# The preparation of a four-layer convolution kernel: projection by column and by row in two strips of 64 array rows

## The chip, the core and the metric

The kernel runs on one core of one Trainium2 chip. A core has five engines that run their own instruction streams: TensorE (matmuls), VectorE, ScalarE, GpSimd and SyncE, which here only issues DMA transfers. The metric is the device time of one execution in microseconds (us); lower is better. Three executions of the kernel before took 5565.35, 5569.03 and 5571.29 us, with a median of 5569.03.

## What is computed

The input x has shape (2, 128, 128, 128): two images, 128 channels, 128 rows, 128 columns, all float32. Four layers follow each other, each as x + layer(group norm of x): an axial attention with relative positions, four directional recurrent convolutions, a deformable convolution, and a Hadamard-transformed convolution. Only the preparation of the first layer is touched. Cut to that part, the reference is:

```python
x = jnp.transpose(x, (0, 3, 1, 2))          # (N, W, C, H)
x = x.reshape(N * W, C, H)                  # one sequence for each column of an image
# qkv: a grouped projection, 8 groups, 16 input and 32 output channels in each group
# q, k: 8 channels of a group each, v: 16; each followed by batch norms whose
# statistics run over all sequences and positions
```

The attention scores of a group are the sum of q·k and of two products with a table of relative positions. Each of the three is normalised with its own mean and variance over all sequences and positions. The preparation must therefore find these moments before the attention can start, and it must leave q, k and v behind in device memory.

## The kernel before, in words

`layer0_prepare` (L92) keeps both images in on-chip memory as `xa[n]`, with the 128 channels on the partitions and rows x columns (128 x 128) along the free dimension. The projection weights are block-diagonal: output channel of group g uses only the 16 input channels of group g. `wt` holds them as columns: 256 to 383 are q and k (64 q columns, then 64 k columns, 8 for each group in turn), 384 to 511 are v (16 for each group).

First the images arrive, their Gram matrices are summed, and the group norm and batch norm are folded into the weights. From L295 a loop over k (0: q and k, 1: v) broadcasts the scales and biases to all partitions (`rows`, L304) and makes the folded weights `wz[n]` (L307) on VectorE.

Then two stages follow, each a loop of turns over tiles of RT = 4 columns or rows:

- **By column** (L361 to L452, 64 turns: 2 images x 32). `sequences` (L371) multiplies, for each of 4 columns, the image column `xa[n][:, :, w]` as stationary operand (128 channels x 128 rows; neighbouring rows lie 128 elements apart) by the folded weights (256 columns: q, k, v). VectorE adds the biases while it takes the results out of PSUM: q and k go to `zb`, v goes to `vs`, which is written to device memory every fourth turn. `moments` (L400) multiplies `zb` by itself in 16 small matmuls of 32 columns; ScalarE copies one half of the result, VectorE multiplies it by the other, GpSimd sums up.
- **By row** (L456 to L569, 33 turns). `positions` (L466) multiplies, for each of 4 rows and both images, the image row `xa[n][:, h, :]` (128 elements side by side) by the q and k weights (128 columns). VectorE adds the bias into `zt`. `against_embeddings` (L489) multiplies `zt` by itself in 32 small matmuls into `pg`, which VectorE multiplies by the table `eg`. From turn 4 on, `project` (L512) also writes q and k themselves: the weights are stationary, 16 x 32 pixels move, ScalarE takes the result out twice (`sa`, `sb`), and SyncE writes it to device memory.

TensorE, VectorE and ScalarE go through a wrapper `InOrder` (L73), whose line 81 is therefore the line of nearly all instructions in the profile; the program's order is kept on each engine. In each column turn the order is: matmuls of `sequences` for turn i, then `moments` of turn i - 1. In each row turn: `positions` of turn t, the share of `project`, then `against_embeddings` of turn t - 1. GpSimd's and SyncE's instructions are placed by a scheduler.

[...] By column: `ps_zb` 4 x 1 bank, `ps_m` 2, one for small results. By row: `ps_zt` 2 x 1, `pg` 2, `ps_q` 2, one for small results.

Of the kernel before, what the change touches and what calls it, by code (L numbers as in the profile page):

```python
# [7 lines left out]
F32 = mybir.dt.float32  # L8
I32 = mybir.dt.int32
AF = mybir.ActivationFunctionType  # L10
ALU = mybir.AluOpType
# [4 lines left out]
P = 128  # L16
N = 2
S = 128
RT = 4
# [4 lines left out]
NG = 8  # L24
# [67 lines left out]
def layer0_prepare(env, x, prm, mem, alphas):  # L92
# [4 lines left out]

    nc, tc = env.nc, env.tc  # L100
    HW = WC // 2
    with ExitStack() as ctx:
        xpool = ctx.enter_context(tc.tile_pool(name="l0x", bufs=1, side="right"))
        kp = ctx.enter_context(tc.tile_pool(name="l0k", bufs=1))
        xa = [xpool.tile([P, S, S], F32, name=f"xa{n}", tag=f"xa{n}") for n in range(N)]
        pe, dve, act = (InOrder(tc, e) for e in (nc.tensor, nc.vector, nc.scalar))
# [2 lines left out]
        strip, ones = late[:, 0:128], late[:, 128:256]  # L109
        gsim = kp.tile([P, NG, 3], F32, name="gsim", tag="gsim")  # L110
        rows = kp.tile([P, 2, 1 + N, P], F32, name="rows", tag="rows")
        wz = [kp.tile([P, 2, P], F32, name=f"wz{n}", tag=f"wz{n}") for n in range(N)]
        shift = kp.tile([P, N], F32, name="shift_qk", tag="shift_qk")
        eg = kp.tile([P, 9, S], F32, name="eg", tag="eg")

        with ExitStack() as early:
            wp = early.enter_context(tc.tile_pool(name="l0w", bufs=1))
            pp = early.enter_context(tc.tile_pool(name="l0ps", bufs=1, space=PSUM))
            ct = wp.tile([P, 512], F32, name="ct", tag="ct")
            wt = wp.tile([P, 512], F32, name="wt", tag="wt")  # L120
# [57 lines left out]
            a, b, width = e0, e1, 255  # L178
            for k in range(7):
                step = 1 << k  # L180
                width -= step
                to = eg if k == 6 else b
# [3 lines left out]
                a, b = b, a  # L186
# [24 lines left out]
            ps = pp.tile([P, 2 * N], F32, name="psg_l0", tag="ps_small")  # L211
# [83 lines left out]
            for k in range(2):  # L295
                psr = pp.tile([P, 1 + N, P], F32, name="psr", tag="psr")
                for s in range(2):
                    dgs = wp.tile([P, 1 + N, P], F32, name="dgs", tag="dgs", bufs=2)
                    for c in range(1 + N):
                        nc.vector.tensor_scalar(  # L300
                            dgs[:, c, :], pick[:, k, s, :], cols[:, s, c : c + 1], None, ALU.mult
                        )
                    nc.tensor.matmul(psr, lhsT=ones, rhs=dgs, start=(s == 0), stop=(s == 1))
                nc.scalar.copy(rows[:, k], psr)  # L304
                lo = 256 + 128 * k
                for n in range(N):
                    nc.vector.scalar_tensor_tensor(  # L307
                        wz[n][:, k, :],
                        wt[:, lo : lo + P],
                        gs[:, n : n + 1],  # L310
                        rows[:, k, 0, :],
                        ALU.mult,
                        ALU.mult,
                    )
# [30 lines left out]
        def along(n, k, shape):  # L345
            return (
                rows[:, k, 1 + n, :]
                .rearrange("p (b c) -> p b c", b=(4, NG)[k])
                .unsqueeze(1 if k == 0 else 2)
                .to_broadcast(shape)  # L350
            )
# [9 lines left out]
        with ExitStack() as part:  # L361
# [2 lines left out]
            pp = part.enter_context(tc.tile_pool(name="l0pm", bufs=2, space=PSUM))  # L364
            acc = sp.tile([P, 2, 33], F32, name="acc2", tag="acc2")
            nc.gpsimd.memset(acc, 0.0)
            zb = [sp.tile([P, RT, 4, 33], F32, name=f"zb{j}", tag=f"zb{j}") for j in range(2)]
            for t in zb:
                nc.gpsimd.memset(t[:, :, :, 32:33], 1.0)

            def sequences(i, vs):  # L371

                n, w = i // NT, i % NT * RT
                z = zb[i % 2]
                for hf in range(2):
# [9 lines left out]
                    dve.tensor_tensor(  # L385
                        z[:, 2 * hf : 2 * hf + 2, :, 0:32],
                        ps[:, :, 0, :].rearrange("p w (b c) -> p w b c", b=4),
                        along(n, 0, [P, 2, 4, 32]),
                        ALU.add,
                    )  # L390
                    at = (w + 2 * hf) % HW
                    dve.tensor_tensor(
                        vs[:, :, at : at + 2, :],
                        ps[:, :, 1, :].rearrange("p w (g c) -> p g w c", g=NG),
                        along(n, 1, [P, NG, 2, 16]),
                        ALU.add,
                    )
                return z

            def moments(z):  # L400


                ps = pp.tile([P, 2, 2, 33], F32, name="ps_m", tag="ps_m")
                for half in range(2):
                    for b in range(2):
                        for s in range(4):
                            w, block = 2 * half + s // 2, 2 * b + s % 2
# [12 lines left out]
            z_last = None  # L420
            for i in range(N * NT + 1):
# [34 lines left out]
        with ExitStack() as part:  # L456
# [5 lines left out]
            zt = [sp.tile([P, RT, 4, 33], F32, name=f"zt{j}", tag=f"zt{j}") for j in range(4)]  # L462
            for t in zt:
                nc.gpsimd.memset(t[:, :, :, 32:33], 1.0)

            def positions(t):  # L466

                zs = []
                for n in range(N):
                    z = zt[2 * (t % 2) + n]  # L470
                    ps = pp.tile([P, RT, P], F32, name="ps_zt", tag="ps_zt")
                    for hh in range(RT):
                        pe.matmul(
                            ps[:, hh, :],
                            lhsT=xa[n][:, t * RT + hh, :],
                            rhs=wz[n][:, 0, :],
                            start=True,
                            stop=True,
                        )
                    dve.tensor_tensor(  # L480
                        z[:, :, :, 0:32],
                        ps.rearrange("p h (b c) -> p h b c", b=4),
                        along(n, 0, [P, RT, 4, 32]),
                        ALU.add,
                    )
                    zs.append(z)
                return zs

            def against_embeddings(t, zs):  # L489
                pg = pp.tile([P, RT, 33], F32, name="pg", tag="pg")  # L490
                for hh in range(RT):
                    for n in range(N):
                        for b in range(4):
                            pe.matmul(
                                pg[32 * b : 32 * b + 32, hh, :],
                                lhsT=zs[n][:, hh, b, 0:32],
                                rhs=zs[n][:, hh, b, :],
                                start=(n == 0),
                                stop=(n == N - 1),
                            )  # L500
# [1643 lines left out]
```

## Time and profile before

| what | value |
| --- | --- |
| median of 3 runs | 5569.03 us |
| profiled execution, its own time | 5575.76 us |
| profiled execution, span of its instructions | 5574.0 us |
| TensorE matmuls (PE), busy | 5231.2 us, 94% |
| TensorE weight loads (PEld), busy | 4656.9 us, 84% |
| VectorE (DVE), busy | 3700.6 us, 66% |
| ScalarE (ACT), busy | 2582.8 us, 46% |
| GpSimd (POOL), busy | 1532.4 us, 27% |
| stage by column | 112 to 272 us |
| stage by row | 272 to 423 us |

In the rows of a profile, PE is a matmul record and PEld the weight load that goes with it. One float32 matmul of the program leaves two records of each. "128*128 128x256" means a stationary operand of 128 rows and 128 columns and a moving operand of 256 elements on 128 partitions. Matmuls are pipelined, and the duration of a record includes the time through the array, so the distance from one record's start to the next says more than its duration. A timeline row gives the start, the time from the first start to the last end, the engine, the line, the operation, output<-inputs, the shape and the number of records; in brackets the idle time before it and what ended it. In a tile view the durations are minimum/median/maximum in ns.

### The profile page before, as it was taken

To read this page: it belongs to the slowest core of one execution; us is meant where nothing else is said; L and a number is where in the kernel's file an instruction comes from. 1 tells how busy PE (TensorE), PEld (TensorE's weight loads), DVE (VectorE), ACT (ScalarE), POOL (GpSimd) and SP (SyncE) were. 2 spreads that over 40 slices of the span, in tenths; PEclk is the share of its full clock that TensorE was granted. 3 is DMA by queue.
4 is the path that set the end of the run, shared out by engine and by line. 5 is a ranking of instruction groups with operands and counts; after the bars stand their busy time and mean duration, and the time that the engine had idled before them with its cause. 6 is when DMAs were issued, how large, how long until landed. Compare 5 with 4: busy or idle time off the path is not lost. (4 is left out here: it accounts for less than half of the span.)

```text
span 5574.0 us, 171601 instructions
## 1 busy us (share of the span) xinstructions
PE 5231.2 (94%) x71931; PEld 4656.9 (84%) x71931; DVE 3700.6 (66%) x7132; ACT 2582.8 (46%) x7864; POOL 1532.4 (27%) x1169
## 2 busy tenths in 40 slices
PE   7997999999999806999999999999899999999999
PEld 6866888888888706999999999993699999999877
DVE  3635888888888875555555556663466666666798
ACT  1056988898889743443223330003233333333322
POOL 2114666666666621000000003330000000000376
PEclk8998999999999958999999999999999999999999
DMA  3353333333333389900000000104576777766211
GB/s 152 108 221 85 60 60 60 60 60 61 60 60 63 95 338 186 100 1 1 1 1 1 1 1 32 47 16 119 113 87 89 88 85 88 90 88 88 44 50 58
DMA packets 673352, 420.99 MB, mean 76 GB/s; under 512 B 325696, under 2 KB 630720, under 8 KB 660672
## 3 DMA queue, kind: packets, MB, share of 16 engines
q1 hardware_dynamic: 667406, 400.69, 38.9%
q8 instruction: 576, 9.44, 0.7%
q10 hardware_dynamic: 5170, 9.23, 0.5%
q14 instruction: 200, 1.64, 0.1%
HBM read 269.09 MB, written 157.45 MB: 77 GB/s over the span
## 5 line engine op out<-in xcount | busy, mean ns | idle before, releaser
L81 PE MATMUL pl<-ln,wl 128*128 128x128 f32 (+1 forms) x10160 | 1243.3, 276 | 31.3 <-DVE ln L81 29.9
L81 PEld LDWEIGHTS pl<-ln,wl 128*128 128x128 f32 x10160 | 1178.4, 191 | 43.8 <-ACT c L81 21.3
L81 ACT ACTIVATE e<-e,mx 128x128 f32<-128x128 f32 x2048 | 793.4, 395 | 0.8 <-DVE mx L81 0.8
L81 ACT COPY sm<-ps_s 128x432 f32<-128x432 f32 (+1 forms) x768 | 318.4, 487 | 834.1 <-PE ps_s L81 808.8
L81 POOL TENSOR_TENSOR e<-e,total 128x1024 f32<-128x1024 f32 x256 | 485.8, 1897 | 485.5 <-DVE total L81 474.8
L81 ACT COPY res<-ln 128x128 f32<-128x128 f32 x762 | 261.8, 344 | 747.0 <-DVE ln L81 722.0
L81 DVE COPY s<-ps_w 100x1152 f32<-100x1152 f32 x256 | 346.4, 1353 | 334.6 <-PE ps_w L81 334.6
L81 PE MATMUL ps_s<-s,xw 100*128 100x144 f32 x4096 | 546.8, 287 | 7.6 <-DMA xw<-px_d 7.6
L81 POOL TENSOR_TENSOR res<-ln,x1t 128x128 f32<-128x128 f32 x256 | 149.1, 583 | 1456.0 <-DVE ln L81 1456.0
L81 PE MATMUL po<-sm,wdef 128*128 128x256 f32 x2304 | 539.1, 379 | 0.0
L81 PE MATMUL pl<-ln,ws 128*128 128x128 f32 x4064 | 537.6, 274 | 0.0
L81 POOL COPY et<-et 128x1024 f32<-128x1024 f32 x256 | 516.8, 2019 | 34.9 <-DVE et L81 25.7
L81 PEld LDWEIGHTS ps_s<-s,xw 100*128 100x128 f32 x4096 | 518.7, 191 | 8.2 <-DMA xw<-px_d 8.0
L81 DVE TENSOR_TENSOR v<-pl,c 128x128 f32<-128x128 f32 x508 | 148.0, 291 | 564.8 <-PE pl L81 542.3
L81 PEld LDWEIGHTS pl<-ln,ws 128*128 128x128 f32 x4064 | 495.5, 191 | 0.0
L81 ACT ACTIVATE r<-gen,alphas 128x1536 f32<-128x1536 f32 x256 | 395.0, 1543 | 171.3 <-PE gen L81 142.4
L81 PEld LDWEIGHTS po<-sm,wdef 128*128 128x128 f32 x2304 | 419.8, 190 | 47.7
L81 POOL MEMSET col<- 128x10 f32 (+1 forms) x72 | 5.9, 122 | 1462.0 <-DVE res L81 1454.6
L81 ACT ACTIVATION_READ_ACCUMULATOR e<-e,mx 128x1 f32 x2048 | 396.2, 193 | 0.0
L81 DVE SCALAR_TENSOR_TENSOR ln<-v,res 128x128 f32<-128x128 f32 x1016 | 346.1, 341 | 48.5 <-POOL res L81 0.9
L81 PE MATMUL te<-cst_main,e 128*128 128x128 f32 x2048 | 337.9, 287 | 28.1 <-POOL e L81 20.6
L81 DVE COPY et<-te 128x512 f32<-128x512 f32 x512 | 348.3, 680 | 13.3 <-PE te L81 13.0
(244 smaller groups left out, 9140.4 us busy)
## 6 DMA issues: line engine op xcount, KB each, us to landing
xw<-px_d SPq DMA_DIRECT2D x1275, 80.0 KB
xa<-in_x SPq DMA_DIRECT2D x16, 1024.0 KB
v_d<-vs SPq DMA_DIRECT2D x16, 1024.0 KB
qb_d<-sb SPq DMA_DIRECT2D x16, 1024.0 KB
qa_d<-sa SPq DMA_DIRECT2D x8, 2048.0 KB
zz<-qb_d SPq DMA_DIRECT2D x1024, 16.0 KB
vt<-v_d SPq DMA_DIRECT2D x64, 256.0 KB
qk<-qa_d SPq DMA_DIRECT2D x256, 64.0 KB
```

The costliest lines, as they stand in the source:

```text
L81: return lambda *a, **k: self.tc.keep_in_program_order(issue(*a, **k))
```

## The change

Both projections are cut in two strips of 64 array rows: strip s holds input channels 64s to 64s + 63, and with them groups 4s to 4s + 3. As the weights are block-diagonal, a strip needs only the weight columns of its own four groups. So each matmul becomes two, with 64 rows and half as many moving columns, and the two results lie in two PSUM banks. Around it:

- The folded weights of the strips are a new tile `wzs[n]` (v columns first, then q and k); the old `wz[n]` keeps only q and k, for `project`.
- The q and k bias is reordered by strip on GpSimd (`along_qk`), and repeated four times for the row stage (`by_row`).
- By column the results of a whole turn lie in one tile of two banks (two of them instead of four of one bank). VectorE takes them out in three additions instead of four: two for `zb`, one of 512 elements for `vs`.
- In `moments` ScalarE copies both halves, and the product moves from VectorE to GpSimd.
- By row `ps_zt` holds both images in two banks, two such tiles; `pg` has one buffer instead of two.

```diff
-        wz = [kp.tile([P, 2, P], F32, name=f"wz{n}", tag=f"wz{n}") for n in range(N)]
+        wz = [kp.tile([P, P], F32, name=f"wz{n}", tag=f"wz{n}") for n in range(N)]
+        wzs = [kp.tile([P, 2, 64], F32, name=f"wzs{n}", tag=f"wzs{n}") for n in range(N)]
...
                 for n in range(N):
-                    nc.vector.scalar_tensor_tensor(
-                        wz[n][:, k, :],
...
+                    for s in range(2):
+                        half = slice(64 * s, 64 * s + 64)
...
+                        to = wzs[n][half, 1 - k]
+                        nc.vector.scalar_tensor_tensor(
...
+            for n in range(N):
+                nc.vector.scalar_tensor_tensor(
+                    wz[n], wt[:, 256:384], gs[:, n : n + 1], rows[:, 0, 0, :], ALU.mult, ALU.mult
+                )
+                nc.gpsimd.tensor_copy(
+                    along_qk[n].rearrange("p s (b c) -> p s b c", b=2),
+                    rows[:, 0, 1 + n, :].rearrange("p (b s c) -> p s b c", b=2, s=2),
+                )
+                nc.gpsimd.tensor_copy(
+                    by_row[n], along_qk[n].unsqueeze(2).to_broadcast([P, 2, RT, 64])
+                )
...
-                for hf in range(2):
-                    ps = pp.tile([P, 2, 2, P], F32, name="ps_zb", tag="ps_zb", bufs=4)
-                    for j in range(2):
+                ps = pp.tile([P, 2, 4, P], F32, name="ps_zb", tag="ps_zb")
+                for j in range(RT):
+                    for s in range(2):
+                        half = slice(64 * s, 64 * s + 64)
                         pe.matmul(
-                            ps[:, j],
-                            lhsT=xa[n][:, :, w + 2 * hf + j],
-                            rhs=wz[n],
+                            ps[:, s].rearrange("p g (k w c) -> p k g w c", k=2, w=RT)[:, :, :, j],
+                            lhsT=xa[n][half, :, w + j],
+                            rhs=wzs[n][half].rearrange("p k (g c) -> p k g c", g=4),
...
-                gq = gp.tile([P, 2, 33], F32, name="gq", tag="gq")
-                act.copy(gq, ps[:, :, 0, :])
-                dve.tensor_tensor(gq, gq, ps[:, :, 1, :], ALU.mult)
-                nc.gpsimd.tensor_tensor(acc, acc, gq, ALU.add)
+                gq = gp.tile([P, 2, 2, 33], F32, name="gq", tag="gq")
+                act.copy(gq, ps)
+                nc.gpsimd.tensor_tensor(gq[:, :, 0, :], gq[:, :, 0, :], gq[:, :, 1, :], ALU.mult)
+                nc.gpsimd.tensor_tensor(acc, acc, gq[:, :, 0, :], ALU.add)
...
+                ps = pp.tile([P, 2, RT, N, 64], F32, name="ps_zt", tag="ps_zt")
                 zs = []
                 for n in range(N):
+                    for hh in range(RT):
+                        for s in range(2):
+                            half = slice(64 * s, 64 * s + 64)
+                            pe.matmul(
+                                ps[:, s, hh, n, :],
+                                lhsT=xa[n][half, t * RT + hh, :],
+                                rhs=wzs[n][half, 1],
...
-                pg = pp.tile([P, RT, 33], F32, name="pg", tag="pg")
+                pg = pp.tile([P, RT, 33], F32, name="pg", tag="pg", bufs=1)
...
                 pe.matmul(
                     ps,
-                    lhsT=wz[n][:, 0, :],
+                    lhsT=wz[n],
                     rhs=xa[n][:, b * 16 : (b + 1) * 16, wc * WC : (wc + 1) * WC],
```

More of the change, by code (lines that the diff above doesn't have):

```diff
@@ L111, in layer0_prepare @@
         rows = kp.tile([P, 2, 1 + N, P], F32, name="rows", tag="rows")
-        wz = [kp.tile([P, 2, P], F32, name=f"wz{n}", tag=f"wz{n}") for n in range(N)]
+        wz = [kp.tile([P, P], F32, name=f"wz{n}", tag=f"wz{n}") for n in range(N)]
+        wzs = [kp.tile([P, 2, 64], F32, name=f"wzs{n}", tag=f"wzs{n}") for n in range(N)]
+        along_qk = [kp.tile([P, 2, 64], F32, name=f"aqk{n}", tag=f"aqk{n}") for n in range(N)]
+        by_row = [kp.tile([P, 2, RT, 64], F32, name=f"byr{n}", tag=f"byr{n}") for n in range(N)]
         shift = kp.tile([P, N], F32, name="shift_qk", tag="shift_qk")
@@ L306, in layer0_prepare, with own_groups @@
                 for n in range(N):
-                    nc.vector.scalar_tensor_tensor(
-                        wz[n][:, k, :],
[L309 to L314, printed above, removed]
+                    for s in range(2):
+                        half = slice(64 * s, 64 * s + 64)
+                        def own_groups(a):
+                            if k == 1:
+                                return a[half, half]
+                            return a[half].rearrange("p (b s c) -> p b s c", b=2, s=2)[:, :, s]
+                        to = wzs[n][half, 1 - k]
+                        nc.vector.scalar_tensor_tensor(
+                            to if k == 1 else to.rearrange("p (b c) -> p b c", b=2),
+                            own_groups(wt[:, lo : lo + P]),
+                            gs[half, n : n + 1],
+                            own_groups(rows[:, k, 0, :]),
+                            ALU.mult,
+                            ALU.mult,
+                        )
[9 more added lines that the diff above has]
+                    by_row[n], along_qk[n].unsqueeze(2).to_broadcast([P, 2, RT, 64])
+                )
             psq = pp.tile([P, 1 + N], F32, name="psq", tag="ps_small")
@@ L343, in logit_scales @@
             nc.vector.tensor_tensor(alphas[:, :, to], t3, gsim[:, :, to], ALU.mult)
[L345 to L351, printed above, removed]
         pe, dve, act = (InOrder(tc, e) for e in (nc.tensor, nc.vector, nc.scalar))
@@ L384, in sequences, with both @@
                         )
-                    dve.tensor_tensor(
-                        z[:, 2 * hf : 2 * hf + 2, :, 0:32],
-                        ps[:, :, 0, :].rearrange("p w (b c) -> p w b c", b=4),
-                        along(n, 0, [P, 2, 4, 32]),
+                def both(k):
+                    return ps[:, :, :, 64 * k : 64 * k + 64].rearrange(
+                        "p s g (w c) -> p (s g) w c", w=RT
+                    )
+                for e in range(2):
+                    dve.tensor_tensor(
+                        z[:, :, :, 16 * e : 16 * e + 16].rearrange("p w j c -> p j w c"),
+                        both(1)[:, e::2],
+                        along_qk[n]
+                        .rearrange("p s (j c) -> p (s j) c", j=4)[:, e::2]
+                        .unsqueeze(2)
+                        .to_broadcast([P, 4, RT, 16]),
                         ALU.add,
                     )
[L391 to L397, printed above, removed]
+                at = w % HW
+                dve.tensor_tensor(
+                    vs[:, :, at : at + RT, :],
+                    both(0),
+                    rows[:, 1, 1 + n, :]
+                    .rearrange("p (g c) -> p g c", g=NG)
+                    .unsqueeze(2)
+                    .to_broadcast([P, NG, RT, 16]),
+                    ALU.add,
+                )
                 return z
@@ L406, in moments @@
                         for s in range(4):
-                            w, block = 2 * half + s // 2, 2 * b + s % 2
+                            w, block = 2 * half + s // 2, 2 * (s % 2) + b
                             pe.matmul(
@@ L461, in layer0_prepare @@
             nc.gpsimd.memset(acc, 0.0)
-            zt = [sp.tile([P, RT, 4, 33], F32, name=f"zt{j}", tag=f"zt{j}") for j in range(4)]
+            zt = [sp.tile([P, 2, RT, 2, 33], F32, name=f"zt{j}", tag=f"zt{j}") for j in range(4)]
             for t in zt:
-                nc.gpsimd.memset(t[:, :, :, 32:33], 1.0)
+                nc.gpsimd.memset(t[:, :, :, :, 32:33], 1.0)
             def positions(t):
+                ps = pp.tile([P, 2, RT, N, 64], F32, name="ps_zt", tag="ps_zt")
                 zs = []
                 for n in range(N):
-                    z = zt[2 * (t % 2) + n]
[L471 to L479, printed above, removed]
+                    for hh in range(RT):
[5 more added lines that the diff above has]
+                                rhs=wzs[n][half, 1],
+                                start=True,
+                                stop=True,
+                            )
+                    z = zt[2 * (t % 2) + n]
                     dve.tensor_tensor(
-                        z[:, :, :, 0:32],
-                        ps.rearrange("p h (b c) -> p h b c", b=4),
-                        along(n, 0, [P, RT, 4, 32]),
+                        z[:, :, :, :, 0:32].rearrange("p s h b c -> p (s h) b c"),
+                        ps[:, :, :, n, :].rearrange("p s h (b c) -> p (s h) b c", b=2),
+                        by_row[n].rearrange("p s h (b c) -> p (s h) b c", b=2),
                         ALU.add,
@@ L495, in against_embeddings @@
                                 pg[32 * b : 32 * b + 32, hh, :],
[L496 to L497 removed]
+                                lhsT=zs[n][:, b % 2, hh, b // 2, 0:32],
+                                rhs=zs[n][:, b % 2, hh, b // 2, :],
                                 start=(n == 0),
```

## The prediction, made before the changed kernel was run

> **What bounds the kernel now.** I read the busy time by stage first, since only the preparation is edited. It has two stages that the change touches: the projection by column (112 to 272 us, L371 to L438) and by row (272 to 423 us, L466 to L558).
>
> ```profile
> core 0: us, PE busy (x) PEld busy (x) DVE busy (x) ACT busy (x) POOL busy (x), PEclk, DMA share, GB/s
> 112.00:272.00 160.00, 158.23 (x2560) 140.28 (x2559) 110.11 (x324) 13.80 (x64) 21.11 (x67) 0.99 0.31 103
> 272.00:423.00 151.00, 144.57 (x2690) 101.33 (x2690) 60.97 (x143) 83.83 (x129) 17.71 (x40) 0.99 0.53 211
> ```
>
> TensorE is busy 99% and 96% of the two stages, at a granted clock of 0.99; VectorE has 69% and 40%. In the waits of both stages TensorE waits for another engine 7 us in all (1.0 by column; 3.7, 2.0 and 0.2 by row). So a microsecond of TensorE is a microsecond of the span, here and nowhere else: nothing after 423 us is edited.
>
> Next, what TensorE spends a turn on: the timelines of one turn of each stage, and of one piece of the attention.
>
> ```profile
> 193.35 0.46 PE L81 MATMUL ps_m<-zb 128*32 128x33 f32 x32
> 193.74 2.13 PE L81 MATMUL ps_zb<-wz,xa 128*128 128x256 f32 x8
> 195.80 0.39 PE L81 MATMUL ps_m<-zb 128*32 128x33 f32 x23
> ...
> 347.38 2.05 PE L81 MATMUL ps_zt<-wz,xa 128*128 128x128 f32 x16
> 349.27 1.88 PE L81 MATMUL ps_q<-xa,wz 128*128 128x512 f32 x4
> ...
> 1003.89 1.04 PE L81 MATMUL lg<-cst_main,r 128*128 128x128 f32 x8
> 1004.86 1.16 PE L81 MATMUL lg<-qk 8*128 8x128 f32 x16
> ```
>
> A column turn takes 195.80 - 193.35 = 2.45 us; 64 of them are 157 of the 160 us. Every f32 matmul is two records, each with a weight load of its own. The third piece is the nearest thing to the change: lg<-qk alternates between two strips of array rows, each record with a fresh 128-column load.
>
> Last, the tile views, for the loads:
>
> ```profile
> L81 PEld LDWEIGHTS ps_zb<-wz,xa x512: 291/303/333, 111.6 to 268.8; 128*128 128x128 f32 x171
> L81 PE MATMUL ps_zb<-wz,xa x512: 379/383/797, 111.6 to 269.0; 128*128 128x256 f32 x171
> ...
> L81 PEld LDWEIGHTS ps_zt<-wz,xa x512: 186/192/337, 272.5 to 415.0; 128*128 128x128 f32 x171
> L81 PE MATMUL ps_zt<-wz,xa x512: 275/275/466, 272.5 to 415.1; 128*128 128x128 f32 x171
> ...
> L81 PEld LDWEIGHTS po<-sm,wdef x2304: 187/190/193, 3977.9 to 5219.4; 128*128 128x128 f32 x192
> ```
>
> This carries the forecast. Both projections load 128 columns of the image as weights. By row (ps_zt) they lie side by side: 192 ns. By column (ps_zb) consecutive ones are 128 elements apart: 303 ns, and at the least 291. It is not the wider moving operand, as po<-sm,wdef also moves 256 elements and loads in 190. From record to record, ps_zt takes 0.1115 us (16 of them between 347.38 + 0.11 for the first load and 349.27) and ps_zb 0.22 us (2.13 less 0.38 for the last record and 0.2 for the first load, over 7). A load thus occupies its strip about 0.11 us side by side and about 0.11 + (303 - 192 ns) = 0.22 us strided: **each stage is paced by its weight loads as much as by its matmuls.** The change shortens the matmuls and doubles the number of loads.
>
> **The change, part by part.**
>
> Column projection, per turn. Removed: 4 matmuls of 256 elements (8 records x 0.22 = 1.76 us). Added: 8 of 128 elements on 64 rows (16 records), in two strips. What a pair of strip records costs is not in the trace for 64 rows and a strided load. From below: lg<-qk issues 8 pairs, whose loads start between 1004.86 and 1005.64 (0.97 us of weight loads less the last one's 0.19), 0.11 us a pair; so strips of 8 rows do overlap, load and matmul. From above: no overlap of loads, 2 x 0.22 = 0.44. I take 0.22, one strided load, as the nearest row is the same load of the same tile and strips read different partitions. Eight pairs are 1.76, as before; only the last matmul, which no load follows, is shorter: 383 - 275 = 108 ns. 64 x 0.108 = **-6.9 us**.
>
> Row projection, per turn (32). Removed: 8 matmuls of 128 elements (16 records x 0.1115 = 1.78). Added: 16 of 64 elements (32 records, 16 pairs). At one load of 0.11 a pair this is 1.76 to 1.78 again. The last matmul moves 64 elements instead of 128: 275 ns against 196 ns for the 33-element pg is 0.83 ns an element, 64 x 0.83 = 53 ns; 32 x 0.053 = **-1.7 us**. The upper end, no overlap, is +1.78 a turn.
>
> A new change of array shape. Today ps_q follows ps_zt in the same 128-row shape and its load hides: 349.27 is just where ps_zt's last record ends. After, ps_q follows 64-row strips. The lg piece has such a step (128 rows to strips): eight records 0.109 apart from 1003.89 would put the ninth at 1004.76; the first strip load starts at 1004.86 and its matmul one load later, 1004.97. So 0.21 us, in the 28 turns that have both (t from 4 to 31): **+5.9 us**. The steps to pg and ps_m and back exist today.
>
> VectorE per column turn: 2 x 425 + 2 x 414 + 224 = 1.90 us become 2 x 425 + 692 (a 512-element add, zt's row) = 1.54. This removes nothing from the end, as TensorE's turn of 2.34 stays longer. The z adds now wait for the whole turn's matmuls, but moments of a turn are issued a turn later: 2 x 0.425 lies beside 1.76. If TensorE's turn fell below 1.54, VectorE would set it.
>
> ScalarE and GpSimd. The copy of ps_m grows from 66 to 132 elements: 215 ns against 487 for 432 is 0.74 ns an element, +0.05 us; the product moves to GpSimd, at the 326 ns of its 66-element sum, 0.65 us a turn. Beside 2.34 both are hidden, but once, at the end of the stage, the chain to psm is 0.05 + (0.33 - 0.22) longer: **+0.2 us**.
>
> Weights and biases. Ten VectorE products instead of four at L307. Six (at most 6 x 0.35 = 2.1) run in the 2.80 us in which it waits for the second rows copy (0.61 used before). Behind that copy two half-size products precede the first matmul instead of one: between -0.1 and +0.3, taken as 0. GpSimd's four copies: 2.02 us for 1024 elements gives 0.25 and 1.0 us, 2.5 together from 111.2 to 113.7; the first add needs one of them at 113.8, and the first moments, at 117.4, the memsets behind them.
>
> Buffers and queues. pg falls from two to one: prod reads it in 0.39 + 0.15 us, and the next pg comes a row projection (1.8 us) later. In the row stage both images now share their two banks, so VectorE reads one image's half while TensorE writes the other's. No row shows that; between 0 and the read itself, 0.69 us a turn. I take 0. SyncE's transfers keep number, size and place, at 0.31 and 0.53 of the DMA engines.
>
> Sum: -6.9 - 1.7 + 5.9 + 0.2 = **-2.5 us**. The profiled execution took 5575.76 us (span 5574.0); the median of the runs is 5569.03, so I forecast 5569.0 - 2.5 = **5566.5 us**.
>
> [...]
>
> **The rivals.**
>
> A, faster: in strips the strided load costs no more than a contiguous one. Against it: 291 ns even for the first load of a turn, with nothing in flight. For it: no 64-row strided load is in the trace. Pairs then take 0.11: 64 x (8 x 0.108 + 0.108) = 62 us off. TensorE's turn would be 1.5, level with VectorE's 1.54, so about 58. With +4.4 for the rest (5.9 + 0.2 - 1.7): 5569 - 54 = **5515**.
>
> B, slower: the shared banks of ps_zt. TensorE's writes to one image wait while VectorE reads the other. It decides from 0.08 us a turn (2.5/32), and leaves "no change" from 0.42; at the full read of 0.69 it is 22 us, 19.5 with the sum above: **5589**.
>
> C, slower: loads of 64-row strips don't overlap. For it: overlap is shown only for strips of 32 (gen) or 8 rows (lg). 64 x 1.76 + 32 x 1.78 = 170 us, 167 with the sum above: **5736**; if only strided loads collide, 113: 5680.
>
> That the change does nothing to the time is my forecast.
>
> **How the numbers follow.** A measurement tells 0.2%, 11 us, from no change. Forecast 0.52 (its own range 5555 to 5581), A 0.20, B 0.16, C 0.12. The range takes in A and B with some 10 us about them and leaves out C: 5505 to 5597. Of the forecast's 0.52, 0.48 lies within 11 us, 0.02 on either side; B lies half within. So faster 0.20 + 0.02 = 0.22, same 0.48 + 0.08 = 0.56, slower 0.12 + 0.08 + 0.02 = 0.22.
>
> **What would show it.** The load of ps_zb: near 300 ns in 64-row strips is the forecast, near 190 is A. Column turn: 2.34 us (forecast), 1.5 (A), over 4 (C). Row turn with a projection: 4.40 + 0.16 = 4.55; for B TensorE idle at ps_zt. Gap before ps_q's first load: 0.1 us, new. I am wrong if the stretch from 112 to 423 us differs from 311 by more than 11 us.

## The result, and the profile after

The changed kernel takes **5621.73 us** (median of 4 runs, 5618.07 to 5623.04) against 5570.16 us for the kernel before on the same chip (4 runs, 5565.35 to 5574.83). The ratio is **1.0088**, with a 95% interval of 1.0075 to 1.0100: slower. The forecast was 5566.5 us, its range ended at 5597.

I read the stages first. This is the windows view of the kernel after, cut at its own boundaries (first ps_zb, first ps_zt, last pg), with the columns of the same view in the prediction.

```profile
core 0: us, PE busy (x) PEld busy (x) DVE busy (x) ACT busy (x) POOL busy (x), PEclk, DMA share, GB/s
109.40:262.70 153.30, 150.58 (x3074) 140.17 (x3074) 88.24 (x200) 17.18 (x64) 39.57 (x131) 1.00 0.33 109
262.70:468.60 205.90, 175.72 (x3201) 116.53 (x3200) 59.79 (x136) 83.56 (x128) 15.37 (x38) 0.87 0.37 153
```

The column stage fell from 160.9 to 153.3 us, with TensorE as dense as before. The row stage, cut the same way, grew from 148.3 to 205.9 us. Two things are new in its row: TensorE is busy for only 175.72 us of it (85%, where it was 96%), and the granted clock is 0.87. The tail up to the attention is 15.7 us in both kernels. So -7.6 and +57.6 us are the whole result; the spans differ by 45.2, because the first matmul of the stage came 2.2 us earlier and all that follows the attention's first matmul took 2.7 us less in the one profiled execution.

Next, what answers to the timelines and tile views of before. First the column turn of after, TensorE alone:

```profile
190.78 0.46 PE L81 MATMUL ps_m<-zb 128*32 128x33 f32 x32
191.17 2.02 PE L81 MATMUL ps_zb<-wzs,xa 64*128 64x128 f32 x16
193.12 0.46 PE L81 MATMUL ps_m<-zb 128*32 128x33 f32 x32
```

The tile views of after, durations in ns as minimum/median/maximum:

```profile
L81 PEld LDWEIGHTS ps_zb<-wzs,xa x1024: 287/310/310, 109.4 to 258.3; 64*128 64x128 f32 x171
...
L81 PEld LDWEIGHTS ps_zt<-wzs,xa x1024: 182/188/335, 262.7 to 462.7; 64*128 64x128 f32 x171
```

A column turn is 193.12 - 190.78 = 2.34 us, and a strided load is as long in a strip of 64 rows (310 ns) as it was in 128 (303). Now a row turn of after:

```profile
351.45 0.97 PEld L81 LDWEIGHTS ps_zt<-wzs,xa 64*128 64x128 f32 x16
351.45 1.11 PE L81 MATMUL ps_zt<-wzs,xa 64*128 64x64 f32 x16
...
352.61 0.69 DVE L81 TENSOR_TENSOR zt<-ps_zt,byr 128x512 f32<-128x512 f32 x1 [0.53 <-PE ps_zt L81]
...
353.35 0.97 PEld L81 LDWEIGHTS ps_zt<-wzs,xa 64*128 64x128 f32 x16 [0.93 <-DVE zt L81]
353.35 1.11 PE L81 MATMUL ps_zt<-wzs,xa 64*128 64x64 f32 x16 [0.79 <-DVE zt L81]
354.39 0.30 PEld L81 LDWEIGHTS ps_q<-xa,wz 128*128 128x128 f32 x2
...
357.00 1.11 PE L81 MATMUL ps_zt<-wzs,xa 64*128 64x64 f32 x16
```

TensorE issues the first image's 16 strip records and then stops. VectorE's addition of that image starts at 352.61, when the last record is out of the array, and ends at 353.30; only then, at 353.35, does the second image begin. The weight loads stand still for 0.93 us: 0.19 from the end of the last load (352.42) to the addition, 0.69 for the addition, 0.05 to the next load. The turn is 357.00 - 351.45 = 5.55 us. Before it was 4.40, from 347.38 (the prediction's line) to the next turn's first row:

```profile
351.78 0.49 PE L81 MATMUL ps_zt<-wz,xa 128*128 128x128 f32 x2
```

The waits of the stage say how often, after:

```profile
PEld ps_zt L81 <- DVE zt L81: 32.2, 32, 3.2
PE ps_zt L81 <- DVE zt L81: 27.6, 32, 3.0
```

and before:

```profile
PEld ps_zt L81 <- DVE zt L81: 0.5, 1, 0.5
PE ps_zt L81 <- DVE zt L81: 0.2, 1, 0.2
```

That is once in every turn, where it was a single wait.

### The profile page after: what moved, and what is told of

Read it like the earlier page. It is cut to its first block, busy times and chain, and to the rows that moved or that the text cites. A ratio compares the mean times of both kernels' runs of the same rounds, so it can differ in the third digit from the quotient of the medians.

```text
span 5619.2 us, 173471 instructions
## 1 busy us (share of the span) xinstructions
PE 5253.6 (93%) x72955; PEld 4672.3 (83%) x72955; DVE 3681.0 (66%) x7010; ACT 2585.5 (46%) x7864; POOL 1552.2 (28%) x1237
## 5 line engine op out<-in xcount | busy, mean ns | idle before, releaser
L81 DVE TENSOR_TENSOR v<-pl,c 128x128 f32<-128x128 f32 x508 | 148.3, 292 | 564.4 <-PE pl L81 542.2
```

The lines of the kernel that those rows point to most:

```text
L81: return lambda *a, **k: self.tc.keep_in_program_order(issue(*a, **k))
```

## The experiments

Theory W (wait): the second image's matmuls wait for the first image's addition, as both images have one tile of two banks. Theory H (clock): what is left is the granted clock, which goes by how long moving operands stream through the array and not by how long TensorE is occupied. Rivals: the strips themselves are slower by row (loads, changes of shape), or the two strip edits disturb each other. "Stage" is first ps_zb to first ps_zt, and from there to the last pg; "half" is the time at a granted clock of 0.5 inside the row stage. Ratios are against the kernel before on the same chip, with 95% intervals.

| kernel | median us | ratio | column | row | half |
| --- | --- | --- | --- | --- | --- |
| before | 5570.16 | 1 | 160.9 | 148.3 | 3.4 |
| after | 5621.73 | 1.0088 (1.0075 to 1.0100) | 153.3 | 205.9 | 54.6 |
| column_only | 5569.16 | 0.9987 (0.9978 to 0.9996) | 153.2 | 148.8 | 3.4 |
| row_only | 5635.62 | 1.0106 (1.0090 to 1.0121) | 161.6 | 208.1 | 58.0 |
| both_first | 5590.21 | 1.0025 (1.0016 to 1.0034) | 153.8 | 171.0 | 35.4 |
| own_banks | 5592.56 | 1.0030 (1.0019 to 1.0041) | 153.4 | 171.9 | 34.1 |
| side_by_side | 5627.11 | 1.0089 (1.0074 to 1.0105) | 153.3 | 211.0 | 64.9 |
| wide_moving | 5581.27 | 1.0014 (1.0005 to 1.0023) | 153.3 | 158.9 | 3.4 |
| early | 5578.80 | 1.0005 (0.9996 to 1.0014) | 153.3 | 159.7 | 17.1 |
| fill_long | 5613.58 | 1.0072 (1.0056 to 1.0087) | 153.8 | 197.3 | 32.7 |
| fill_full | 5621.73 | 1.0086 (1.0070 to 1.0103) | 153.3 | 204.6 | 34.1 |
| first_fill | 5593.69 | 1.0033 (1.0020 to 1.0045) | 153.3 | 176.2 | 17.1 |
| column_contig | 5538.81 | 0.9933 (0.9919 to 0.9946) | 127.1 | 149.2 | 6.1 |
| before_contig | 5567.48 | 0.9983 (0.9974 to 0.9992) | 150.3 | 149.1 | 3.4 |
| column_early | 5563.66 | 0.9978 (0.9969 to 0.9987) | 153.2 | 143.5 | 3.4 |
| before_early | 5569.81 | 0.9990 (0.9980 to 0.9999) | 160.5 | 143.5 | 3.1 |

### Each strip edit alone: column_only, row_only

column_only takes `positions`, `zt`, `along` and `pg` from the kernel before; row_only takes `sequences` from it.

> Only the column stage in strips; the row stage as before the change. The row stage is then 148 us again. Theory W: only the column stage's gain is left, 149.0 us of ps_zb instead of 157.4, so 8 us less than before: some 5562 us. Rival S: the column stage's strips cost something that the stage windows hide (a lower clock behind it, a later start): 5570 or more.

> Only the row stage in strips as in the changed kernel; the column stage as before. Theory W: the whole loss stands here, 58 us more than before: some 5628 us, with the wait of ps_zt for zt in every turn and a clock of 0.9. Rival S gives the same time. If the loss needs both stages (for instance through the POOL work or the v transfers that the column stage leaves behind), it is below 5600.

The edits add up within the intervals: 0.9987 and 1.0106 make 1.0093, after has 1.0088. No sign is left that they disturb each other, and the loss lies in the row stage alone. The column strips give 7.6 us, and the measurement, 0.13%, is just on that side of no change.

### The wait: both_first, own_banks, side_by_side

both_first issues both images' matmuls ahead of the two additions:

```diff
                 ps = pp.tile([P, 2, RT, N, 64], F32, name="ps_zt", tag="ps_zt")
-                zs = []
                 for n in range(N):
                     for hh in range(RT):
...
+                zs = []
+                for n in range(N):
                     z = zt[2 * (t % 2) + n]
```

own_banks gives each image a tile of its own, two banks half used:

```diff
+                    banks = pp.tile([P, 2, 512], F32, name="ps_zt", tag="ps_zt")
+                    ps = banks[:, :, 0:256].rearrange("p s (h c) -> p s h c", h=RT)
```

side_by_side keeps the one tile and gives each image one half of a bank instead of interleaving them:

```diff
-                ps = pp.tile([P, 2, RT, N, 64], F32, name="ps_zt", tag="ps_zt")
+                ps = pp.tile([P, 2, N, RT, 64], F32, name="ps_zt", tag="ps_zt")
```

> The changed kernel, but in each row turn TensorE gets the matmuls of both images before VectorE's two additions, which take no result while the other image's matmuls are still to come. Theory W (the 52 us are a wait in the row stage: the second image's matmuls stand in the same two banks as the first image's, so they wait for its addition; the granted clock falls because of that idle time): TensorE no longer waits for zt (59.8 us of waits before), the clock of the row stage is back at 0.99, a row turn with two projections takes 4.40 + 0.16 = 4.56 us; total some 5565 us (column stage 8 less than before, row stage 3 more). Rival S (64-row strips themselves are dear in the row stage, by the steps between array shapes or by a lower clock): the wait goes, but the total stays above 5600 and the clock near 0.9.

> The changed kernel with the order of its instructions kept; each image's row results have two banks of their own (half filled), the two images' tiles taking turns in the same four banks. Theory W: as before the change, an image's matmuls wait only for its own addition a turn earlier; no idle time, clock 0.99, total some 5565 us, equal to the run with both images first within 3 us. Rival S: above 5600. If this run gains and the other doesn't, it is not the order but the sharing of banks that costs.

> After, with the two images in the two halves of each bank of ps_zt, side by side instead of interleaved: image 0 writes the first 256 elements of a bank, image 1 the last 256. If the wait between the images goes by bank, it stays: 32 waits of TensorE for the addition, row stage near 206 us, 1.0088 of the kernel before. If it goes by the addresses that are written and read, the wait goes: row stage near 171, 1.0025 to 1.003, as in both_first.

Theory W holds: with either edit the wait is gone (own_banks keeps one, of 1.7 us) and the row stage falls by 35 and 34 us. In both_first the timeline has a turn with a projection in 354.91 - 350.37 = 4.54 us, 1.01 less than after, and all 32 strip records in one go:

```profile
350.37 0.76 PE L81 MATMUL pg<-zt 128*32 128x33 f32 x64
...
353.00 1.99 PE L81 MATMUL ps_q<-xa,wz 128*128 128x512 f32 x4
354.91 0.77 PE L81 MATMUL pg<-zt 128*32 128x33 f32 x64
355.61 2.00 PE L81 MATMUL ps_zt<-wzs,xa 64*128 64x64 f32 x32
```

side_by_side keeps the wait (32 times, 32.0 us on the weight loads): images that share no address of a bank still wait for each other. Whether the wait goes by the bank or by the tile isn't separated, as own_banks changes both.

But the expectation for both_first and own_banks was missed: some 22 us of the loss stayed (171.0 against the 148.8 of column_only).

### The clock: wide_moving, early, fill_long, fill_full, first_fill

This is the windows view of both_first, in the row turns before the first projection:

```profile
265.00:283.00 18.00, 18.00 (x327) 17.43 (x328) 7.78 (x24) 0.21 (x1) 1.36 (x8) 0.50 0.09 28
```

TensorE is busy 18.00 of 18.00 us, and the clock is 0.50 throughout. It came back only with the projections, after a stretch of 27.3 us. A clock that went by how long TensorE is busy would not stay there. So I changed what it does, not how long it is busy. wide_moving is own_banks with the strips moving 128 elements instead of 64 (v too, whose results nobody reads); the loads are the same:

```diff
-                                rhs=wzs[n][half, 1],
+                                rhs=wzs[n][half].rearrange("p k c -> p (k c)"),
```

early is both_first with the projections from turn 1 on, not 4:

```diff
-            wait = 4
+            wait = 1
```

fill_long is after with one matmul of 64 rows in the gap, whose result nobody reads; fill_full is the same with 128 rows:

```diff
+                    if n == 0:
+                        idle = small.tile([P, 512], F32, name="idle", tag="psm")
+                        pe.matmul(
+                            idle,
+                            lhsT=xa[0][0:64, t * RT, :],
+                            rhs=xa[0][0:64, 0:4, :],
```

first_fill is both_first with four such matmuls of 128 rows, unread too, in each of turns 0 to 3 (`if t < 4:`).

> The run with own banks, but each strip matmul of the row stage moves 128 elements instead of 64 (the v columns too, whose results nobody reads): the loads are the same, the moving stream is twice as long. After the runs without the wait, 20 us are still lost in the row stage, and the granted clock stands at 0.5 for the first 25 us of it, as long as there are no projections. Theory H (the clock gate goes by how long the moving operand streams; a 64-element strip matmul behind a 128-column load streams half of the time, so a clock that has fallen stays low until the projections come; and the loads pace the records): a warm turn keeps its 4.54 us but for 0.05, the clock is up again within 7 us of the stage's start, and the total is 13 us below own_banks. Rival R (64 rows in use as such keep the clock low): no change of the clock, total as own_banks. Rival P (the matmuls pace, not the loads): the turn grows by 16 x 0.053 = 0.85 us, and the total by 25.

> The run with both images first, but projections start in turn 1 instead of turn 4 (two in each turn, where it was three in six turns). Theory H: the long-streaming projections bring the clock up within 7 us of the stage's start, 15 us less than both_first. Rival R: the clock of the first turns stays at 0.5 and the projections run at half speed there: as both_first or slower.

> After, with one more matmul between the two images' strips in each row turn, 128 columns of weights and 512 elements to move, whose result nobody reads; the wait of the second image for the addition stays. At full clock this matmul takes some 0.9 us (ps_q's 512-element records: 1.88 us for 4), about the 0.93 us that TensorE waits. Theory (wait and clock are two separate costs, and the clock goes by the share of time in which an operand streams): the turn stays as long as in after, but the half clock of the row stage falls from 54.6 us to below 20, so the row stage is 148.3 + 30 + 5 = 183 to 190 us against 205.9: 1.005 to 1.006. Rival (the clock falls for another reason than the wait and the short strips): the half clock stays above 40 us and the added matmul is paid for, row stage 206 to 235, 1.009 to 1.014.

> fill_long with one thing changed: the matmul in the gap has 128 rows instead of 64 (same 512 elements, same records, result unread). In fill_long TensorE stays at half clock from 265 us until the projections come, although the 64-row fill streams for 1.7 of each 6.35 us there. If the clock goes by how much of the array streams (rows as well as time), the full-height fill lifts it: half clock of the row stage from 32.7 us to below 15, row stage 197 to some 186, 1.005 of the kernel before. If it goes by time alone, whatever the rows, nothing changes: 32.7 us, 197, 1.007.

> both_first, with four more matmuls of 512 elements and 128 rows in each of the first four row turns, the turns without projections; their result is unread. At full clock they take 4 x 4 x 0.86 = 13.7 us. Theory (the clock comes back when what moves streams for some three quarters of the time or more): at half clock a turn would be 3.6 strips + 1.0 pg + 6.8 added = 11.5 us, of which about 1.7 + 0.9 + 6.8 = 9.4 stream, 82%; fill_full, where it did not come back, has 63% by the same count, and early, where it did after 10.2 us, 74%. So the half clock at the start of the row stage should fall from 27.3 us to 3.4 or 10.2, and the stage should be 171.0 - 8 to 12 + 13.7 = 173 to 177 us. Rival (what is added in the gap does not count, only the strips or the projections do): half clock until the projections, 27 us and the added 13.7 twice, some 45 to 50 us, stage 195 to 200.

wide_moving streams twice as much, and its row stage is 13.0 us shorter than that of own_banks (0.16% by the runs, some 9 us): the clock is back after 3.4 us, and a warm turn (at full clock) costs 4.59 us instead of 4.54, so the loads, not the stream, pace the strips. That sank both rivals: the clock came back with 64 rows in use, and the turn did not grow by 0.85. early gains 11.3 us, but it says less of the clock than its expectation did: 5.3 of them are what the spreading gives with the row stage as before (column_early below, 148.8 to 143.5), and the stretch at half clock lasted 10.2 us, not 7. The fills were half a miss. In fill_long the turn stays at 5.55 us while the gap is full, as the timeline shows,

```profile
352.00 0.77 PE L81 MATMUL pg<-zt 128*32 128x33 f32 x64
352.69 1.11 PE L81 MATMUL ps_zt<-wzs,xa 64*128 64x64 f32 x16
353.63 1.07 PE L81 MATMUL idle<-xa 64*128 64x512 f32 x2
354.59 1.11 PE L81 MATMUL ps_zt<-wzs,xa 64*128 64x64 f32 x16
...
357.55 0.65 PE L81 MATMUL pg<-zt 128*32 128x33 f32 x52
```

and after's seven later drops of 3.4 us, which make a turn up to 1.7 us longer (7.24 for 5.55), are gone: 8.6 us less in the stage. But the first stretch stayed: 34.1 us at half clock, in fill_long as in fill_full, against 30.7 in after. Neither "below 20" nor "above 40" was right, and the height of the fill made no difference to that stretch. fill_full even lost 7 us more, 0.19 us in a turn at full clock (5.74 for 5.55) and 0.50 at half. The second image's strips start 2.01 us behind its fill at half clock (271.85 to 273.86) and 1.01 behind that of fill_long, so the fill of the full height does not seem to run beside strips.

What was left of theory H was the share of time. I count, as an estimate, 0.83 ns an element at full clock (the prediction's figure from ps_zt and pg) and twice that at half (four ps_q records of early take 3.70 us at half clock and 1.98 at full). At half clock a turn without projection streams 1.7 (strips) + 0.9 us (pg) of 4.65 in both_first: 55%. fill_full has 63% by the same count, fill_long 68% at most (4.3 of 6.35 us), early 74% in the turn with its first projections, wide_moving over 90%. If that is the quantity, the clock returns somewhere above 63 to 68% and by 74%. first_fill, at 82%, would show if not. Its windows view:

```profile
266.00:276.00 10.00, 10.00 (x53) 5.68 (x52) 2.69 (x6) 0.00 (x0) 0.43 (x6) 0.72 0.00 1
276.00:286.00 10.00, 10.00 (x186) 6.01 (x184) 2.35 (x7) 0.00 (x0) 0.46 (x1) 1.00 0.02 3
```

The clock is back 6.8 us after it fell, before any projection; 13.7 us of added work cost the stage 5.2 us (176.2, expected 173 to 177). Theory H holds for coming back, in that form. For staying up it doesn't take as much: the column strips stream about 0.107 of every 0.22 us, 49%, and keep a clock of 1.00 through 153 us.

The averages of turns hide what the traces say step by step, as the clock of these traces is 0.5 or 1.0 and changes on a grid of 3.41 us (stretches at half clock of 3.4, 6.8, 10.2, 27.3, 30.7 and 34.1 us). early comes back, at 274.5, behind a step that its first projections fill:

```profile
271.00 3.70 PE L81 MATMUL ps_q<-xa,wz 128*128 128x512 f32 x4
```

But fill_long has steps of over 0.8 by the same count and stays at half; its added stream is the one that uses 64 rows alone. So I weight each record's stream by the share of the array's rows and columns that it uses, an estimate from the times and shapes of the matmul records and the same 0.83 ns. In the column and row stages of all 16 traces each of the 57 returns then follows a step of 0.72 or more, and the 64 steps behind which the clock stayed at half have 0.71 or less, in fill_full up to 0.71, in fill_long up to 0.56. Each of the 50 falls follows a step of 0.38 or less, and of the 1334 steps behind which the clock stayed up none has less than 0.35; the column strips of after have 0.43 to 0.48 in all but one. This is a count over runs that were made for other ends. No run was made to fail it, and the height alone is not isolated, as the clock stayed at half behind both fills. With the stream at the start of its record instead of its end the bounds are 0.75 (one step that stayed at half has 0.76), 0.37 and 0.34.

### The loads: column_contig, before_contig

Both take image rows instead of columns as stationary operand in the column stage, so the q, k and v of that stage are those of rows. column_contig is column_only with the edit, before_contig the kernel before.

```diff
-                            lhsT=xa[n][half, :, w + j],
+                            lhsT=xa[n][half, w + j, :],
```

> column_only, but in the column stage the stationary operand is row w of the image instead of column w, so that the 128 loaded elements lie side by side (q, k and v of the column stage are then those of rows). Loads that pace, and are slow for their stride: the load falls from 310 to 188 ns, a pair of strip records from 0.22 to 0.11 us, a turn from 2.34 to some 1.55 us, where VectorE (1.54) comes in: 50 us less than column_only. If the stride isn't the cause, the same time.

> The kernel before the change, with that same edit of the column stage (row w in place of column w; its q, k and v are then those of rows). Here the load hides behind a matmul of 256 elements (0.215 us), so only the first load of a turn and 5 ns a record are saved: a turn of 2.30 instead of 2.45, 8 to 10 us less than before. If the column stage were paced by the loads far more than by its matmuls, 25 us or more less.

The tile view of column_contig:

```profile
L81 PEld LDWEIGHTS ps_zb<-wzs,xa x1024: 182/188/335, 114.0 to 235.2; 64*128 64x128 f32 x171
```

Side by side the same load takes 188 ns instead of 310, and a turn falls from 2.34 to 1.48 us (183.18 to 184.66 below). So the stride sets the price of the pair, as the prediction had it, and two strips do run beside each other. In full-height form the same edit gains 10.6 us in the profile and 0.17% by the runs (expected: 8 to 10 us); in strips the stage gains 26.1 us. A turn of before_contig takes 182.54 - 180.22 = 2.32 us:

```profile
180.22 0.46 PE L81 MATMUL ps_m<-zb 128*32 128x33 f32 x32
...
182.54 0.46 PE L81 MATMUL ps_m<-zb 128*32 128x33 f32 x32
```

So strips are worth something where the matmul, not the load, is the longer one: 1.48 against 2.32 us.

The expected 50 us came to 30 by the runs, which lie between 5530 and 5550 us (the profile is of the slowest), and the reason is one that I hadn't named:

```profile
183.18 0.46 PE L81 MATMUL ps_m<-zb 128*32 128x33 f32 x32
183.56 1.16 PE L81 MATMUL ps_zb<-wzs,xa 64*128 64x128 f32 x16
184.66 0.46 PE L81 MATMUL ps_m<-zb 128*32 128x33 f32 x32
185.05 1.16 PE L81 MATMUL ps_zb<-wzs,xa 64*128 64x128 f32 x16
186.14 0.25 PE L81 MATMUL ps_m<-zb 128*32 128x33 f32 x2
187.58 0.45 PE L81 MATMUL ps_m<-zb 128*32 128x33 f32 x30 [1.19 <-issue]
```

TensorE stops for up to 2.5 us in the middle of a group of matmuls, with nothing that the profile shows to wait for ("issue"): 14.1 us of weight-load idle ahead of ps_m and 7.0 ahead of ps_zb. Another 14.5 us went at half clock, which costs at most half of that.

### The best version: column_early, before_early

column_early is column_only with the projections from turn 1 (`wait = 1`); before_early is the kernel before with that edit.

> Column projection in strips, row projection as before, and the projections of the row stage spread over turns 1 to 32 instead of 4 to 32. The column stage should stay at 153.2 us. The row stage before has 13.2 us in which TensorE waits for ScalarE's copy sb in turns with many projections, and 3.4 us of half clock; spreading should take a part of the first, some 4 to 9 us: row stage 140 to 145 against 148.8, in all 0.997 to 0.998 of the kernel before. Rival: the projections then compete with the first turns and only move the same work, so row stage 148.8 and 0.9987, as with the column strips alone.

> The kernel before with the projections spread over turns 1 to 32, nothing else. If what column_early gains over the column strips alone comes from the spreading alone, the row stage here falls by the same amount (4 to 9 us, to 140 to 145 us) with the column stage at 160.9, and the two changes add up. Rival: 148.3, no gain.

Both expectations were met: both row stages fall to 143.5 us, and the two edits add up: 0.9987 and 0.9990 against 0.9978 (0.9969 to 0.9987) together. The waits of ps_q's weight loads for ScalarE's sb fall from 9.5 to 0.9 us. column_early, 5563.66 us where the kernel before takes 5574.13, is the fastest kernel here that computes the whole.

## Why the prediction was wrong, point by point

- **Column stage, "I take 0.22, one strided load": right.** Load 310 ns, turn 2.34 us as forecast, -7.6 us for -6.9. Rival A fell with it: its condition, a load near 190 ns, holds only where the image lies side by side (188 ns in column_contig).
- **Row stage, one load of 0.11 a pair: right.** Turns in which nothing waits are 4.54 us (both_first) for a forecast of 4.55. Rival C, loads that don't overlap, did not occur.
- **The new change of shape, +5.9, less the -1.7 of the shorter last matmul: right in size.** 28 x (4.54 - 4.40) = 3.9 us at full clock, for 4.2. wide_moving, where the last matmul is not shorter, has 0.19 instead of 0.14 a turn, so both terms are seen: 0.21 and 0.053 were forecast. One reading behind it was wrong: 349.27 is not where ps_zt's last record ends (347.38 + 2.05 = 349.43) but one step of 0.11 us behind its start. That the load of ps_q hides there holds all the same.
- **Buffers, "In the row stage both images now share their two banks, so VectorE reads one image's half while TensorE writes the other's ... I take 0": this step failed.** It priced the sharing as contention of two accesses, between nothing and the read. What happens is that the second access isn't made: the second image's matmuls wait for a signal of the first image's addition, in each of 32 turns. So the strip records' way out of the array and the signals in both directions are paid with the read: 1.01 us a turn (5.55 against 4.54), over the upper end of 0.69. Rival B had the place and the engine, at 0.16, but the price of the read alone.
- **The granted clock: no step had it.** The sum took the row turn's records at full clock, which put a term of some 20 us at nothing without a reason. Halving the streams while the loads stay (192 and 188 ns) halves the streaming share of the strips, by the estimate of 0.83 ns from 0.106 to 0.053 us of every 0.11; and once the clock has fallen, as it does at the start of the row stage in the kernel before too (3.4 us), it stays down until the projections come (30.7 us in after, 27.3 in both_first).
- **VectorE, ScalarE, GpSimd, weights, one pg at next to nothing: right as far as the waits show.** Both kernels have the same 15.7 us behind the stage, and column_only has before's row stage within 0.6 us. **SyncE at nothing: but for one turn.** In after's first row turn the first image's addition waits 1.24 us for the write of v, and the second image with it (3.0 us in all).

The row stage, step by step, each step a run: 148.8 (column_only) to 158.9 in wide_moving, +10.1: 28 x (4.59 - 4.40) = 5.3 and four single turns longer by 1.0, 0.6, 1.5 and 2.0 us, less 0.7 in the first; to 171.0 in both_first, +12.1, the clock (half clock 3.4 to 35.4 us): 8.6 in the five turns before the projections have brought it back, 4.8 in two late turns, less 0.05 in the others; to 197.3 in fill_long, +26.3, the wait (32 x 1.01 = 32.3, less 6.0 us net: single longer turns that only both_first has, 10.2, against 4.2 more in fill_long, most of it in the first five turns); to 205.9 in after, +8.6, the clock that the waits cost (half clock 32.7 to 54.6). Of the 57.1 us about half is the wait, a good third the clock.

## What to carry over

Before an operation is cut in strips, compare the weight load with the matmul, at the stride that the load has: here the strips halved what moves and left the load as it was (303 and 310 ns by column, 192 and 188 by row). In both_first that left a stream that filled an estimated 55% of a turn at half clock, with which the clock, once fallen, stayed at 0.50 for 27.3 us. When two producers get one PSUM tile, look in the order of each engine whether the second is issued behind a consumer of the first; issue both producers first, or give each its own banks, and price the wait as drain plus read plus signals (1.01 us a turn here), not as the read (0.69).

## What the runs showed of the hardware

- **Occupied is not streaming.** At half clock TensorE was busy 18.00 of 18.00 us and stayed there; four matmuls of 512 elements a turn brought the clock back in 6.8 us. By the weighted count above, an estimate, it came back behind steps of 0.72 and more and fell behind steps of 0.38 and less, which fits the 49% that kept it up in the column stage, and the later drops of 3.4 to 6.8 us in the row stages of both_first and early (behind steps of 0.17 to 0.22, in which TensorE also stopped). No run tests these bounds.
- **A load's stride costs, in 64 rows as in 128:** 310 against 188 ns in strips, with 0.22 against 0.11 us from pair to pair, and 303 against 190 ns in 128 rows (before_contig).
- **TensorE's stops without a releaser coincide with instruction transfers.** In column_contig all twelve stops of 0.9 us or more between 130 and 238 us begin 0.1 to 1.7 us after the start of a 16 KB packet of the instruction queue (at 186.4, for one, behind a packet at 185.2), though nine of the 21 such packets go by without a stop. This is its transfers view from 185 to 187.5 us:

```profile
## 3 DMA queue, kind: packets, MB, share of 16 engines
q1 hardware_dynamic: 211, 0.20, 24.9%
q8 instruction: 1, 0.02, 2.4%
```

The three longer stops of wide_moving (318.4, 394.6 and 413.7 us) sit behind such packets as well (316.9, 393.5, 413.1). No run took these transfers away, so whether they cause the stops was not shown.
